# Graph layers of a four-layer network: edges from a node to itself are added from the unit's own vectors instead of being gathered

## The chip, the cores and the metric

The kernel runs on one core of a Trainium2 chip. The metric is the device time of one execution in microseconds; of the kernel before, 23 runs are shown, with a median of 2807.59 us (2790.01 to 3037.0). The core has five engines with a queue each: TensorE (PE, its weight loads shown apart as PEld), VectorE (DVE), ScalarE (ACT), GpSimd (POOL) and SyncE (SP). Transfers run on 16 DMA engines; POOL issues the gathers and SP nearly all the rest.

## The reference

The input is `x` of 8 batches x 2048 nodes x 128 features, and one adjacency matrix of 2048 x 2048 for all layers: random, symmetric, with some 16 neighbours per node, and with every diagonal element set. Four layers follow each other, attention (MHA), graph attention (GAT), MHA, GAT:

```python
_a = jax.random.bernoulli(jax.random.fold_in(_gk, 2), 0.00390625, (2048, 2048))
_a = jnp.logical_or(_a, jnp.swapaxes(_a, -1, -2))
_a = jnp.logical_or(_a, jnp.eye(2048, dtype=bool))

# MHA layer: 8 heads of 16, mask = (adj == 0), softmax over the neighbours, then
x = _layer_norm(h + (attn_out @ Wo + bo), ln1_g, ln1_b)
x = _layer_norm(x + relu(x @ W1 + b1) @ W2 + b2, ln2_g, ln2_b)

# GAT layer
h = x @ W
e = (h @ a_src)[:, :, None] + (h @ a_dst)[:, None, :]
e = jnp.where(e >= 0, e, 0.2 * e)
e = jnp.where(adj[None, :, :] == 0, -jnp.inf, e)
out = jnp.einsum('bij,bjd->bid', softmax(e), h)
x = layer_norm(out + x)          # gamma, beta
```

## The kernel before

**Units and slots.** The nodes are cut into 32 units of 64, each unit in two groups of 32. On the 128 partitions a unit is two halves of the batch (4 batches each) by 64 nodes. A unit's edges lie in 1152 slots, 9 tiles of 128: four pairs of tiles, in which each group has one tile of a pair, and a ninth tile that both groups share. The loops run over units and, in a unit, over five steps `t` (four with two tiles, one with one).

**Lists (`block_list`, `unit_list`).** For each of 16 blocks of 128 rows of the adjacency matrix, VectorE turns the row into falling column numbers (L1134), takes maxima until up to 40 neighbours of each node are listed (L1152, L1171), and a chain of small matmuls and ScalarE copies finds where each node's edges begin. For each unit, one-hot matrices `hot` (slot by node, and node by slot) are made, and for every slot the neighbour's number: `idx` (L1369), with the number of rows, 2048, where the slot is empty. A gather with the bound `nodes - 1` leaves out such rows. `empty` holds 1e30 for an empty slot and 0 for others; `owner` holds the number of the slot's node within its group. The lists are made ahead of layer 0 and between its units.

**Tables and gathers (`project`, `gather`).** As each unit leaves a layer, `project` multiplies it by the next layer's weights and stores rows in a table in HBM. A row holds one node for all 8 batches: keys and values for MHA (8192 bytes), and for GAT the score, 128 features and a one, per batch (4160 bytes). The other score of a GAT layer, which belongs to the target node, stays on chip in `t` (`spread_out`, L1665). `gather` (L1763) issues one indirect DMA per tile on POOL, 288 per layer, into a buffer of the pool `kv` (6 buffers; a GAT buffer holds four tiles).

**A GAT layer (`graph`, `opened_graph`, `after_graph`).** `opened_graph` multiplies `hot` by `t` (L2126), so that every slot has its target's score, and subtracts `empty` in `mask` (L2141 to L2150). For each step VectorE adds the gathered score and takes the leaky maximum (`score`, L2065, L2072), ScalarE takes the exponential (L2077), VectorE multiplies it into the one-hot matrix (`fold`, L2087), and TensorE multiplies the gathered features with it and sums per node in PSUM (`add`, L2103). The one in each row gives the sum of the weights as a 129th column. Even units accumulate in two of the four banks of the tile `q`, odd units in the bank `acc` and one of the three shared banks `m`. After the last step `after_graph` takes the inverse of the sums (`inverse`, L2174, L2175), scales the accumulator into `a` (L1732, L1734), multiplies the unit's own `x` by a centring matrix (`centred`, L1567: x less its mean, so that the norm needs no mean), adds the two into `r` (L2193), and goes on with `norm`, `scaled`, `keep` and `project`. The last unit of a layer goes through this in two halves.

**An MHA layer (`attention`).** TensorE spreads the queries over the slots (L1824), VectorE multiplies them with the gathered keys (L1836) and sums per head (L1843), ScalarE takes the exponential (L1853), POOL, and in some steps VectorE, weighs the values (L1869), TensorE sums per node (L1921).

**What sets the order.** No loop issues instructions. Every piece of work is an `Op` with a key (its due place), costs in us per engine that may take it, and the cells that it reads, writes, joins, holds or shares. `Plan.order` runs through the whole program once with these costs, a model of the DMA queues (bytes by a rate) and the counts of buffers, and gives each engine a fixed order; `Plan.issue` then makes the instructions in that order. A cost that is altered in one place can so alter the order of the whole program.

## Time and profile before

| | |
|---|---|
| median of 23 runs | 2807.59 us |
| profiled execution, its own time | 2799.18 us |
| its span (first to last instruction) | 2797.5 us |
| busy: PE, PEld | 2228.5 us (80%), 1359.6 us (49%) |
| busy: DVE, ACT, POOL | 2258.0 us (81%), 1474.8 us (53%), 2086.4 us (75%) |
| DMA | 1022.64 MB, mean 366 GB/s |
| gathers (software queue) | 864.44 MB, 78.2% of the 16 engines' span |
| granted TensorE clock, mean | 0.909 |

A group in the profile is a line, an engine, an operation and its operands by the program's names (`out<-in`), with their shapes, the count, the busy time, the mean of one, and the idle time of the engine just before it with the work that ended it. A stage's row gives busy time per engine, the granted clock of TensorE, the busy share of the DMA engines (by the packets' own times, so it can stand a little over 1) and the rate. fp32 matmuls are recorded as two each.

### The profile page before, as it was taken

To read this page: it belongs to the slowest core of one execution; us is meant where nothing else is said; L and a number is where in the kernel's file an instruction comes from. 1 tells how busy PE (TensorE), PEld (TensorE's weight loads), DVE (VectorE), ACT (ScalarE), POOL (GpSimd) and SP (SyncE) were. 2 spreads that over 40 slices of the span, in tenths; PEclk is the share of its full clock that TensorE was granted. 3 is DMA by queue.
4 is the path that set the end of the run, shared out by engine and by line. 5 is a ranking of instruction groups with operands and counts; after the bars stand their busy time and mean duration, and the time that the engine had idled before them with its cause. 6 is when DMAs were issued, how large, how long until landed. Compare 5 with 4: busy or idle time off the path is not lost. (4 is left out here: it accounts for less than half of the span.)

```text
span 2797.5 us, 61433 instructions
## 1 busy us (share of the span) xinstructions
PE 2228.5 (80%) x22816; PEld 1359.6 (49%) x22816; DVE 2258.0 (81%) x3674; ACT 1474.8 (53%) x4995; POOL 2086.4 (75%) x1447
## 2 busy tenths in 40 slices
PE   6568778778889886888777888888888988677775
PEld 4424443334444445666664344444444444566664
DVE  8699999989999995555555998899999998576665
ACT  6546655566555554655553354555555554454443
POOL 1188888788888877667664888788888886777774
PEclk8888999999999998999996899999999999888887
DMA  7798999889999989999998999999999997999996
GB/s 284 275 361 332 352 354 350 322 353 365 360 409 393 390 305 361 413 408 407 403 409 318 363 371 364 354 413 380 362 403 380 376 401 279 375 407 409 400 396 266
DMA packets 248067, 1022.64 MB, mean 366 GB/s; under 512 B 39184, under 2 KB 52880, under 8 KB 175856
## 3 DMA queue, kind: packets, MB, share of 16 engines
q0 software_dynamic: 166464, 864.44, 78.2%
q1 hardware_dynamic: 81296, 154.18, 14.8%
q8 instruction: 183, 3.00, 0.4%
q14 instruction: 124, 1.02, 0.1%
HBM read 978.23 MB, written 88.08 MB: 381 GB/s over the span
## 5 line engine op out<-in xcount | busy, mean ns | idle before, releaser
L1763 POOL DMA_INDIRECT kv<-table,idx x1152 | 1196.3, 1038 | 520.1 <-issue 274.1
L1869 POOL TENSOR_TENSOR kv<-kv,ex 128x2048 f32<-128x2048 f32 (+1 forms) x242 | 876.0, 3631 | 57.7 <-ACT ex L1853 53.6
L1836 DVE TENSOR_TENSOR kv<-qe,kv 128x2048 f32<-128x2048 f32 (+1 forms) x320 | 662.4, 2070 | 94.1 <-DMA kv<-table,idx 59.0
L1843 DVE TENSOR_REDUCE s<-kv 128x128 f32<-128x2048 f32 (+1 forms) x320 | 660.8, 2065 | 16.1
L1824 PE MATMUL qe<-q_sb,hot 32*128 32x512 f32 (+1 forms) x2304 | 394.3, 686 | 167.5 <-DVE kv L1836 163.8
L1921 PE MATMUL acc<-kv,hot 128*32 128x512 f32 (+1 forms) x2304 | 365.5, 650 | 69.6 <-POOL kv L1869 60.2
L2103 PE MATMUL acc_q<-kv,w 128*32 128x129 f32 (+1 forms) x4608 | 201.5, 312 | 109.5 <-DVE w L2087 97.3
L2087 DVE TENSOR_TENSOR w<-hot,e 128x512 f32<-128x512 f32 (+1 forms) x384 | 222.0, 598 | 73.0 <-ACT e L2077 59.4
L1853 ACT ACTIVATE ex<-s 128x128 f32<-128x128 f32 (+1 forms) x320 | 95.5, 299 | 313.1 <-DVE s L1843 273.7
L1824 PEld LDWEIGHTS qe<-q_sb,hot 32*128 32x128 f32 (+1 forms) x2304 | 104.5, 192 | 320.9 <-DVE kv L1836 243.8
L2103 PEld LDWEIGHTS acc_q<-kv,w 128*32 128x32 f32 (+1 forms) x4608 | 160.0, 128 | 143.4 <-DVE w L2087 114.4
L2065 DVE TENSOR_TENSOR e<-te,kv 128x16 f32<-128x16 f32 (+1 forms) x320 | 58.0, 181 | 192.8 <-DMA kv<-table,idx 190.5
L1543 ACT COPY trows<-ps_p 128x258 f32<-128x258 f32 (+1 forms) x237 | 111.3, 474 | 104.6 <-PE ps_p L1627 40.7
L1921 PEld LDWEIGHTS acc<-kv,hot 128*32 128x32 f32 (+1 forms) x2304 | 54.7, 114 | 228.3 <-issue 108.1
L2077 ACT ACTIVATE e<-e 128x16 f32<-128x16 f32 (+1 forms) x320 | 65.0, 212 | 191.0 <-DVE e L2072 183.8
L1597 PE MATMUL ps_f<-x,W 128*128 128x512 f32 (+1 forms) x264 | 147.9, 645 | 21.5 <-ACT x L1742 13.3
L2103 PE MATMUL acc<-kv,w 128*32 128x129 f32 (+1 forms) x2304 | 114.9, 299 | 57.8 <-DVE w L2087 50.1
L1581 PE MATMUL ps_y<-W,hidden 128*128 128x128 f32 x1024 | 158.4, 276 | 0.0
L1554 PEld LDWEIGHTS ps_t<-ident,normed 128*128 128x128 f32 x638 | 77.4, 154 | 126.2 <-issue 49.2
L1581 PEld LDWEIGHTS ps_y<-W,hidden 128*128 128x128 f32 x1024 | 136.8, 193 | 1.6 <-issue 1.5
L1554 PE MATMUL ps_t<-ident,normed 128*128 128x128 f32 x638 | 122.1, 313 | 17.7 <-ACT normed L1732 8.9
L1699 ACT ACTIVATE junk<-ps_y 128x128 f32<-128x128 f32 x248 | 68.8, 277 | 126.6 <-PE ps_y L1581 113.4
(221 smaller groups left out, 4122.7 us busy)
## 6 DMA issues: line engine op xcount, KB each, us to landing
x<-xd SPq DMA_DIRECT2D x96, 256.0 KB
xd<-xnew SPq DMA_DIRECT2D x93, 256.0 KB
kv<-table,idx POOLq DMA_INDIRECT x1152
table<-trows SPq DMA_DIRECT2D x128, 130.0 KB
kv<-adj_dram SPq DMA_DIRECT2D x16, 1024.0 KB
table<-trows SPq DMA_DIRECT2D x32, 512.0 KB
table<-trows SPq DMA_DIRECT2D x64, 256.0 KB
kv<-xk_dram SPq DMA_DIRECT2D x8, 1024.0 KB
```

Source lines behind the costliest of these rows:

```text
L1543: e.copy(out, in_)
L1554: e.transpose(ps.tile[:, b * P : (b + 1) * P], flat(x.tile)[:, b * P : (b + 1) * P], self.ident)
L1581: e.matmul(ps.tile[:, cols], lhsT=of, rhs=w, start=first and b == 0 and k == 0, stop=last and b == count - 1 and k == len(terms) - 1, skip ...
L1597: lambda e: e.matmul(ps.tile, lhsT=w, rhs=x.tile, start=True, stop=True),
L1763: e.indirect_dma_start(out=rows(kv.tile, j), out_offset=None, in_=self.tables[n][0:nodes], in_offset=bass.IndirectOffsetOnAxis(ap=self.idx ...
L1824: e.matmul(qe.tile[:, j, hf, :], lhsT=hot.tile[rows, t * P : (t + 1) * P], rhs=q.tile[rows, :], start=True, stop=True,)
L1836: e.tensor_tensor(k, qe.tile[:, 0:tiles].rearrange("p j h c -> p (j h) c"), k, ALU.mult)
L1843: e.tensor_reduce(s.tile[:, 0 : tiles * heads].rearrange("p (q c) -> p q c", q=2 * tiles), k, axis=mybir.AxisListType.X, op=ALU.add,)
L1869: e.tensor_tensor(v, v, w.unsqueeze(3).to_broadcast([P, 2 * tiles, heads // 2, HD]), ALU.mult)
L1921: e.matmul(out[rows, :], lhsT=hot.tile[:, col : col + GROUP * (3 - tiles)], rhs=rhs[:, 2 * j + hf, :], start=(t == 0), stop=(t == TG - 1),)
L2087: e.tensor_tensor(w.tile[:, :, j : j + tiles, :].rearrange("p x j c -> p j x c"), oh[:, j : j + tiles].unsqueeze(2).to_broadcast(shape), e ...
L2103: e.matmul(acc(b)[at : at + GROUP * (3 - tiles), :], lhsT=w.tile[:, hf * hb + b, j : j + 3 - tiles, :].rearrange("p j c -> p (j c)"), rhs= ...
```

## The change

- In the lists, VectorE multiplies the block of the adjacency matrix that lies on the diagonal by the identity and sums it, so that each node has a flag for its own edge (`seen[:, 4]`). The flag travels with the node's list and ends as `alone`: 0 with an own edge and -1e30 without.
- In `unit_list`, a second index `others` is made beside `idx`: the slot's neighbour is compared with the slot's own node, and the slot counts as empty if they agree. `empty` is made from it as well, so it now masks such slots. To compare within a unit, the nodes of its second group are numbered 33 to 64 (`number`, `target`).
- `gather` takes `others` in GAT layers and `idx` in MHA layers. The plan's bytes per tile are 113 rows for GAT instead of 120.
- In `project`, when the next layer is GAT, VectorE adds the node's two scores and `alone` into `own`. In `opened_graph` it takes the leaky maximum of it, and ScalarE the exponential.
- `inverse` adds `own` to the sum of the weights, and makes a second column, the inverse times `own`.
- `centred` becomes `mixed_products`: the unit's `x` is multiplied by a matrix of 256 columns, the layer's weights on the left and the centring matrix on the right. An even unit's products go into banks 2 and 3 of its own tile `q`, an odd unit's into two of the banks `m`.
- The addition of `r` becomes, for each batch, `a = product * (own / sum) + a`, and for each pair of batches `r = centred + a`.
- To make room, layer 2's key and value weights take layer 0's tile, both GAT layers use one tile for the turned weights and one for the 256 columns, and `ones` is narrower.

```diff
         self.empty = self.const.tile([P, self.NU, TILES], F32, name="empty")
+        self.others = self.const.tile([P, self.NU, TILES], I32, name="others")
+        self.alone = self.const.tile([P, self.NU], F32, name="alone")
+        self.own = self.const.tile([P, self.NU, self.HB], F32, name="own")
...
-        self.centre = const.tile([P, P], F32, name="centre")
+        self.turned = const.tile([P, P], F32, name="turned")
+        self.mixed = const.tile([P, 2 * P], F32, name="mixed")
+        self.centre = self.mixed[:, P:]
...
-                base=1,
+                base=1 + g % 2 * GROUP,
...
+        op({"ACT": 0.3}, lambda e: e.copy(self.mixed[:, 0:P], wx[:, 1 : P + 1]), key - 400, reads=[at], writes=[self.mixed_at])
...
         def parts(e, q):
+            if q == 0:
+                e.scalar_tensor_tensor(
+                    cand.tile.rearrange("p q c -> p (q c)"),
+                    buf.tile[:, i * P : (i + 1) * P].bitcast(I32),
+                    0.0,
+                    self.ident,
+                    ALU.not_equal,
+                    ALU.mult,
+                    accum_out=self.seen[:, 4, i : i + 1],
+                )
...
+            e.copy(aux16.tile[:, wide : wide + 1], self.seen[:, 4, i : i + 1])
...
+            e.activation(
+                self.alone[:, u : u + 1], ps.tile[:, wide : wide + 1], AF.Identity, bias=self.minus_huge, scale=1e30
+            )
...
+            other = rank.tile[:, 1]
+            e.tensor_tensor(other, rank.tile[:, 0], ps_l.tile[:, 0:TILES, DEG + 2], ALU.add)
+            own = float(self.N - u * UNIT + 1)
+            e.scalar_tensor_tensor(other, other, own, rank.tile[:, 0], ALU.not_equal, ALU.mult)
...
         def indices(e):
-            e.activation(self.idx[:, u], rank.tile, AF.Identity, bias=self.rows_n, scale=-1.0)
-            e.activation(self.empty[:, u], ps_l.tile[:, 0:TILES, DEG + 2], AF.Relu, bias=self.huge, scale=-1e30)
+            e.activation(self.idx[:, u], rank.tile[:, 0], AF.Identity, bias=self.rows_n, scale=-1.0)
+            e.activation(self.others[:, u], rank.tile[:, 1], AF.Identity, bias=self.rows_n, scale=-1.0)
+            e.activation(self.empty[:, u], rank.tile[:, 1], AF.Relu, bias=self.huge, scale=-1e30)
...
-    def centred(self, x, key, *out):
-
-        ps = self.bank("ps_c")
+    def mixed_products(self, x, key, outs, *out):
+
         count = len(self.blocks)
+        if len(outs) == 1 and count == self.HB:
+            made, pairs = outs, [lambda k=k: outs[0].tile[:, 2 + k, :].rearrange("p (b d) -> p b d", b=2) for k in range(2)]
+        else:
+            made = [self.bank("ps_c", [P, 2, 2 * P]) for _ in range(count // 2)]
+            pairs = [lambda ps=ps: ps.tile for ps in made]
+        self.mixed_in = made
 
         def run(e):
             for b in range(count):
-                cols = slice(b * P, (b + 1) * P)
-                e.matmul(ps.tile[:, cols], lhsT=flat(x.tile)[:, cols], rhs=self.centre, start=True, stop=True)
+                e.matmul(
+                    pairs[b // 2]()[:, b % 2, :],
+                    lhsT=flat(x.tile)[:, b * P : (b + 1) * P],
+                    rhs=self.mixed,
...
+                def own_scores(e, ps=ps, v=v):
+                    e.scalar_tensor_tensor(
+                        self.own[:, u, 2 * v : 2 * v + 2],
+                        rows.tile.rearrange("p (b d) -> p b d", b=hb)[:, 2 * v : 2 * v + 2, 0],
+                        self.alone[:, u : u + 1],
+                        ps.tile[:, :, P + 1],
+                        ALU.add,
+                        ALU.add,
+                    )
+
+                self.op({"DVE": 0.17}, own_scores, key, reads=[ps, rows, self.ends_at[u]], **{kind: [self.own_at[u]]})
...
+        idx = self.idx if LAYERS[n] is MHA else self.others
...
-            dma=120 * tiles * width * 4,
+            dma=(120 if LAYERS[n] is MHA else 113) * tiles * width * 4,
...
-                e.tensor_scalar(rc.tile[:, 2 * k : 2 * k + 2], sums, 1e-30, None, ALU.max)
-            e.reciprocal(rc.tile, rc.tile)
+                e.scalar_tensor_tensor(
+                    rc.tile[:, 2 * k : 2 * k + 2, 0], sums, 1e-30, own[:, 2 * k : 2 * k + 2], ALU.max, ALU.add
+                )
+            e.reciprocal(rc.tile[:, :, 0], rc.tile[:, :, 0])
+            e.tensor_tensor(rc.tile[:, :, 1], rc.tile[:, :, 0], own, ALU.mult)
...
-        ps = self.centred(mine, key, r, a)
-        op(
-            {"DVE": 0.65},
-            lambda e: e.tensor_tensor(r.tile, ps.tile, flat(a.tile), ALU.add),
+        pairs = self.mixed_products(mine, key, outs, r, a)
+
+        def residual(e):
+            for k, ps in enumerate(pairs):
+                for b in range(2 * k, 2 * k + 2):
+                    e.scalar_tensor_tensor(
+                        a.tile[:, b, :], ps()[:, b % 2, 0:P], rc.tile[:, b, 1:2], a.tile[:, b, :], ALU.mult, ALU.add
+                    )
+                cols = slice(2 * k * P, (2 * k + 2) * P)
+                e.tensor_tensor(
+                    r.tile[:, cols].rearrange("p (b d) -> p b d", b=2),
+                    ps()[:, :, P:],
+                    a.tile[:, 2 * k : 2 * k + 2, :],
+                    ALU.add,
+                )
+
+        op({"DVE": 0.5 * len(blocks)}, residual, key - 2, reads=[rc, *self.mixed_in], writes=[r, a])
```

## The prediction

> **What bounds the kernel now.** I read the page first (its forty slices show four stages of different make-up), then the busy time by stage, then the groups of instructions within one graph stage, then the packet records. The gathers start at 140 us; the last rows of a graph layer are gathered from 1056 to 1508 us (layer 1) and from 2372 to 2784 us (layer 3), by the first and last 4160-byte packet. Attention fills 140 to 1040 and 1560 to 2300. Busy time by stage (columns: PE, PEld, DVE, ACT, POOL busy, granted TensorE clock, share of the 16 DMA engines, GB/s):
>
> ```profile
> core 0: us, PE busy (x) PEld busy (x) DVE busy (x) ACT busy (x) POOL busy (x), PEclk, DMA share, GB/s
> 140.00:700.00 560.00, 436.98 (x3373) 218.31 (x3374) 524.97 (x667) 327.80 (x1054) 466.62 (x251) 0.92 0.90 348
> 700.00:1040.00 340.00, 298.75 (x2393) 151.80 (x2391) 318.12 (x234) 186.06 (x614) 290.70 (x164) 0.97 0.96 378
> 1190.00:1260.00 70.00, 58.87 (x917) 47.52 (x917) 36.15 (x131) 38.82 (x138) 45.63 (x44) 0.90 1.02 407
> 1400.00:1470.00 70.00, 55.87 (x886) 44.36 (x886) 37.20 (x132) 40.26 (x140) 47.26 (x46) 0.93 1.03 409
> 1560.00:2300.00 740.00, 641.16 (x5063) 327.76 (x5056) 676.22 (x466) 385.58 (x1276) 623.38 (x356) 0.96 0.96 378
> 2520.00:2590.00 70.00, 50.62 (x904) 42.45 (x904) 46.70 (x151) 34.41 (x137) 52.49 (x51) 0.83 1.02 408
> 0.00:140.00 140.00, 85.26 (x376) 64.40 (x376) 103.54 (x388) 82.52 (x241) 20.34 (x58) 0.85 0.74 280
> ```
>
> The reader is to see two regimes. In the graph stages the DMA engines are full (1.02 to 1.03 in every 70 us slice from 1120 to 1470 and from 2450 to 2730), and VectorE is half to two thirds busy: time there is bytes. In attention VectorE (94%, 94%, 91%) and DMA (0.90, 0.96, 0.96) are both close to full: a microsecond of either costs part of itself. The queue that carries the gathers (packets, MB, share of 16 engines), and VectorE's longest wait in layer 1 from 1120 to 1470 (total us, times, longest):
>
> ```profile
> q0 software_dynamic: 166464, 864.44, 78.2%
> ...
> DVE e L2065 <- DMA kv<-table,idx: 90.2, 62, 3.8
> ```
>
> That wait is for gathered rows. The packet records hold 69856 packets of 4160 bytes (mean 166.6 ns) and as many of 8192 bytes (mean 330 ns): 34928 rows per layer, one per edge, so a slot without an edge makes no packet.
>
> **The change, part by part.** The sum is made against the profiled execution (2799.2 us, span 2797.5); the median of the runs shown is 2807.6, 8.4 above it, and a difference worked out on the one is put on the other.
>
> *Removed rows.* Each node has its own edge, so 2048 of 34928 rows fall out of each graph layer. 2048 x 166.6 ns / 16 engines = 21.3 us per layer, 42.6 in all. The slices at 1.02 and above cover 630 of the 864 us in which graph rows are gathered, so 31.1 us surely lies on the bound; of the 11.5 at the layers' ends (shares 0.95, 0.85, 0.96, 0.64) I count seven tenths, 8. Taken: -39, bounds -42.6 and -31. The 288 gathers per layer and their 1.04 us each on POOL stay.
>
> *Lists of edges (layer 0).* Added on VectorE: one 128x128 product with a sum per block (16), between 143 ns (a sixteenth of the 2285 ns that the 128x2048 one takes) and 278 ns (a MAX8 over 128x128); I take 0.26, the nearer in size, plus 83 ns for reading the sum: 5.5 us. Two 128x9 operations per unit (32); rows 128x16, 185 and 176 ns, 128x8 from PSUM 166: 0.34 per unit, 10.9 us. By the counts of the list's rows, 8 blocks and 9 units fall before 140 us (5.8 us), the rest nearly all before 700 (10.5). ScalarE gets four small copies more (about 0.2 to 0.3 each by the 128x9 row, 302 ns); it is 59% busy there, so I count nothing; without that cover it would be 0.8 us a unit.
>
> *Own scores (in layers 0 and 2, where the next graph layer's table is made).* Two operations of 128x2 out of PSUM per unit, on VectorE; the row above them in the code, 128x8 out of PSUM, takes 158 ns, a 128x16 one 176. At 0.165 they are 10.6 us per layer. They read the finished row, so VectorE's queue waits there for ScalarE's copy, as the row above them already does (10.1 us in 15 waits); what queues behind is attention's multiply. I put nothing more on it. By the count of that row 17 units fall before 700 (5.6 us), the others after (5.0).
>
> A rule of the Trainium skill speaks against these small operations: "VectorE: DVE Perf Modes" (the section on the errata) says that each instruction pays a fixed latency and advises operands of 512 elements or more. Its row here is `rcg<-acc`, 128x2 out of PSUM, 149 ns, nearly all of it fixed. The page's own size, 120 cycles plus the columns at 0.96 GHz from PSUM and 58 from SBUF, is smaller (an estimated 127 ns and 70 ns); by it VectorE's new work in attention would shrink by about a quarter, and the sum would be about -21.
>
> VectorE thus gets 16.1 us more from 140 to 700, 15.6 more in the rest of attention and 5.8 ahead of 140. Of two nearly full resources I let the added time count by the share of idle time that the other has: DMA's 10% against VectorE's 6.3% gives 0.61, so 9.8; in late layer 0 and layer 2 (4% against 6.4 and 8.6%) about 0.35, so 5.5; at the start (26% and 26%) a half, 2.9. Sum +18.2; bounds 0 and 37.5.
>
> *The products with centre and weights side by side.* The rows of layer 1 that carry this (groups from 1120 to 1470: count, busy us, mean ns, idle before; the last two are from its timeline: start, us, line, count):
>
> ```profile
> L1625 PE MATMUL ps_p<-Wkv,xnew 128*128 128x256 f32 x215 | 66.3, 435 | 13.5 <-ACT xnew L1742 12.1 <-ACT a L1732 0.8 <-ACT trows L1543 0.4
> L1567 PE MATMUL ps_c<-centre,x 128*128 128x128 f32 x216 | 33.7, 305 | 0.0
> L2193 DVE TENSOR_TENSOR r<-ps_c,a 128x512 f32<-128x512 f32 x27 | 18.5, 687 | 6.2 <-PE ps_c L1567 6.1
> 1323.65 1.13 PE L1625 MATMUL ps_p<-Wkv,xnew 128*128 128x256 f32 x4
> 1324.62 1.05 PE L1567 MATMUL ps_c<-centre,x 128*128 128x128 f32 x8
> ```
>
> Eight matmuls of 128 columns take 1.05 us, and eight of 256 take twice 1.1: +1.1 us per unit on TensorE, with the same weight loads. Layer 1 runs 26 units (260 `ps_te` matmuls, ten each) in the 350 us from 1120 to 1470: 13.46 us each, TensorE busy 288.4, so 11.1. Afterwards it is 12.2 of 12.8 (13.46 less 0.67 for the rows): 0.6 us of slack where there is 2.4. In layer 3 it is 9.1 of 12.2 before, and 10.2 of 11.5 after. Lower bound 0: the granted clock is 0.90 to 0.95 in these slices of layer 1, and at full clock 11.1 would be 10 to 10.5. Upper bound: all of the 2.4 us slack is needed, 1.8 x 32 = 57 us. I take 0.1 us a unit, 3 us, since in late layer 0 VectorE too runs at 94% beside DMA at 0.96; the bound stays in the range.
>
> *The sums after the gather, VectorE in the graph layers.* Instead of one 128x512 addition (687 ns), four 128x128 and two 128x256 ones. The 128x256 form of the same line takes 0.41 us in the timeline, so a further 256 columns cost 0.28 and 128 take about 0.26 (an estimate from these two): 4 x 0.26 + 2 x 0.41 - 0.69 = +1.2; with two 128x4 operations (0.17 each) +1.5 us a unit. VectorE goes from 7.2 to 8.7 of 12.8 us in layer 1 and from 8.3 to 9.8 of 11.5 in layer 3: hidden under the DMA, nothing counted; uncovered it would be 48 us a layer. At the two layers' ends nothing covers it: half a unit's residual, product and small operations, +1 us each, 2 (0 to 5).
>
> *Edits with one answer, nothing:* the exponential of the own scores (ScalarE, 128x4, about 0.2 us a unit; ScalarE is 62% busy at most in the slices of the graph stages) and the constants set up on POOL and VectorE before the first rows arrive. The weights' copy into the tile that layers 1 and 3 share waits for layer 1's last product, near 1514 us, and is first needed near 2400; the key and value weights of layer 2 go into layer 0's tile, free since 140. If these covers were gone, each is one copy, below 1 us.
>
> Sum: -39 + 18.2 + 3 + 2 = -15.8 us: 2783 for the profiled execution, 2791.8 on the median, said as 2791.
>
> **The rivals.** (1) All of VectorE's new work hides, because attention is paced by the DMA: for it, in layer 2 VectorE waits 25.0 us for rows and only 9.5 for the next cause (`qe`); against it, 94% busy VectorE up to 700. -42.6 + 3: 2768. (2) None of it hides: -39 + 37.5 + 5 = +3.5: 2811. For it, early layer 0; against it, layer 2's 9% of idle VectorE. (3) The slower side: TensorE, with its PSUM banks, becomes layer 1's bound. An even unit's products now go into the other two banks of its own accumulator, which is held until the residual is made; an odd unit takes two of the three shared banks at once, while its second accumulator still has the third. Slack goes from 2.4 to 0.6 us a unit, and TensorE's queue is in order, so a late bank holds everything behind it. It decides when a unit needs more than 1.2 us of slack (0.6 plus 0.1 plus 15.8 / 32). At 1.5 us it gives +26 over the forecast: 2818; at all 2.4, 2846. For it: TensorE already waits 24.4 and 18.0 us in that stretch for `w`. Against it: those waits follow the arrival of rows, and the gated clock gives time back.
>
> The Trainium skill, "Perfetto Trace Analysis" (Identifying the Most-Contended Engine), says that matmul busy time judges TensorE's headroom badly and names the busy share of weight loads instead. That share is 0.68 in the row at 1190 and the change adds no load: by that rule rival 3 would cost nothing, and the sum would be -18.8.
>
> (4) The saving doesn't come: rows are dealt to the 16 engines by slot, the missing ones are scattered, and the fullest engine paces each gather. No gain, costs as above (+23.2): 2831. Against it: a unit has 1091 rows on average and its first eight gathers are full, so its ninth holds about 67 of 128 already, and yet the engines stay at 1.02: several gathers in flight even this out.
>
> **How the numbers follow.** The forecast 0.48, rival 1 0.15, rival 2 0.17, rival 3 0.13, rival 4 0.07. The forecast's own range is 2775 to 2805. With rival 1 below and most of 2 and 3 above, 2765 to 2822 leaves out rival 4 and the far end of 3, about two in ten with what I have not thought of. About 0.2%, 5.6 us, is what a measurement of this kernel can tell from no change. Faster: most of the forecast (0.44), rival 1, and the low ends of 2 and 3 (0.07): 0.66. Same: the forecast's upper end and the middle of 2: 0.12. Slower: 0.22. The order of all work is made anew from the altered costs; that can add some microseconds either way and is in the range.
>
> **What would show it.** 4160-byte packets: 65760 instead of 69856. Layer 1's gathers shorter by about 16 us and layer 3's by 20, DMA still at 1.0 in both. Layer 0 longer by about 13, layer 2 by 4. If DMA in layer 1 falls below 0.98 while TensorE is above 93% busy, it is rival 3; if packets fall but the stretch does not shorten and DMA sinks with TensorE no busier, rival 4. A new order that places attention's multiply badly would make the layers 0 and 2 the place of an error.

## The result, and the profile after

The changed kernel takes 2841.46 us (median of 6 runs, 2837.26 to 2844.45), the kernel before 2804.22 (47 runs): a ratio of 1.0131, 95% interval 1.0109 to 1.0154. It is 37 us slower; the forecast was 2791. Ratios and intervals, here and below, leave out executions in a second, slower state and are not simply the quotient of the two medians shown.

The profiled execution of the changed kernel has a span of 2843.9 us, 46.4 more than before. The table cuts both spans at the first and last gathered row of each layer. The column a1 is the first experiment below, the whole change with two VectorE operations formed otherwise. The forecast column holds the prediction's rounded parts, which add up to -14 instead of -15.8. Times here count from the first instruction; those of rows in the prediction count from the first packet, 10.9 us earlier, which changes no length.

| part of the span, us | before | after | a1 | forecast change |
|---|---|---|---|---|
| to the first row | 131.6 | 129.7 | 130.5 | +3 |
| layer 0 | 898.5 | 968.9 | 910.1 | +13 |
| layer 0 to 1 | 15.0 | 20.6 | 15.8 | |
| layer 1 | 452.1 | 434.3 | 434.5 | -16 |
| layer 1 to 2 | 6.8 | 17.0 | 17.0 | +1 |
| layer 2 | 839.6 | 814.4 | 821.8 | +4 |
| layer 2 to 3 | 17.4 | 17.8 | 15.7 | |
| layer 3 | 412.2 | 409.1 | 409.0 | -20 |
| last row to the end | 24.0 | 32.2 | 32.3 | +1 |

So layer 0 alone loses 70.4 us. The busy time by stage of the changed kernel (columns as before: PE, PEld, DVE, ACT, POOL busy, granted clock, share of the DMA engines, GB/s):

```profile
0.00:140.00 140.00, 83.64 (x378) 62.94 (x378) 111.87 (x424) 86.47 (x269) 21.91 (x62) 0.85 0.78 290
140.00:700.00 560.00, 411.92 (x3045) 203.56 (x3049) 536.37 (x697) 307.69 (x1005) 426.44 (x228) 0.87 0.84 318
700.00:1109.00 409.00, 344.24 (x2698) 175.17 (x2691) 383.52 (x317) 215.49 (x704) 328.35 (x184) 0.94 0.89 352
1270.00:1340.00 70.00, 59.92 (x953) 51.61 (x955) 44.60 (x176) 40.53 (x145) 50.38 (x47) 0.90 1.02 401
1600.00:2380.00 780.00, 684.27 (x5466) 342.76 (x5462) 739.71 (x565) 407.11 (x1353) 678.69 (x388) 0.97 0.99 389
2560.00:2630.00 70.00, 55.17 (x910) 45.23 (x914) 55.24 (x198) 35.14 (x145) 54.23 (x52) 0.83 1.02 396
```

In layer 0 VectorE is now 96 and 94% busy, and the DMA engines fell from 0.90 and 0.96 to 0.84 and 0.89: a microsecond of VectorE there goes nearly straight into the time (b4 below measures it). Yet the arithmetic added there is small. The groups of VectorE from 0 to 1115 us (count, busy us, mean ns, idle before) show which instructions hold the time:

```profile
L1392 DVE SCALAR_TENSOR_TENSOR rank_e<-rank_e 128x9 f32<-128x9 f32 x32 | 43.6, 1364 | 1.1
L1161 DVE SCALAR_TENSOR_TENSOR cand<-kv,ident 128x128 f32<-128x128 int32 x16 | 24.9, 1557 | 0.0
L1714 DVE SCALAR_TENSOR_TENSOR own<-trows,alone,ps_p 128x2 f32<-128x2 f32 x60 | 12.3, 206 | 1.3 <-ACT trows L1572 1.3
```

L1392 is the comparison that makes `others`, L1161 the product with the identity. A 128x9 operation of 1364 ns on average is not work: the shortest of the 32 takes 168 ns, the median one 184, the longest 5304; of the 16 of L1161 the shortest takes 280 ns, the longest 7220. Most of the time of both groups (68.5 us busy) lies in the long ones: 13 comparisons and 4 products take over 600 ns, 61.3 us together. Every one of these 17 ends within 0.16 us of the end of a multiply with which GpSimd weighs values. The timeline (start us, us, engine, line, operation) shows what a long one runs against:

```profile
385.81 7.33 POOL L1921 TENSOR_TENSOR kv<-kv,ex 128x2048 f32<-128x2048 f32 x2
386.07 7.22 DVE L1161 SCALAR_TENSOR_TENSOR cand<-kv,ident 128x128 f32<-128x128 int32 x1
393.22 0.08 DVE L1161 DVE_READ_ACCUMULATOR cand<-kv,ident 128x1 f32 x1
```

VectorE's product starts at 386.07, while GpSimd weighs values (two multiplies, 385.81 to 393.14), and ends at 393.29, 0.15 us after it. It is counted as busy throughout, and VectorE starts nothing else meanwhile. The comparison meets the same:

```profile
753.79 7.32 POOL L1921 TENSOR_TENSOR kv<-kv,ex 128x2048 f32<-128x2048 f32 x2
...
756.23 4.91 DVE L1392 SCALAR_TENSOR_TENSOR rank_e<-rank_e 128x9 f32<-128x9 f32 x1
```

It ends at 761.14, 0.03 us after GpSimd's multiplies. The Trainium skill states the rule behind it ("SBUF — State Buffer", Who interferes with whom): a VectorE instruction with two operands in SBUF contends with a GpSimd instruction that reads SBUF, over a shared port that one of them holds for its whole instruction. The rows above agree, with the end of the one 0.03 and 0.15 us after the end of the other. They add that a wait can outlast one instruction: both began under one multiply and ended with the next, which had followed directly.

In the graph layers, the rows that answer those shown of before: the gathers' queue (packets, MB, share) and VectorE's wait for rows from 1200 to 1550 us; below them the groups of the products there.

```profile
q0 software_dynamic: 166464, 847.42, 76.1%
...
DVE e L2117 <- DMA kv<-table,others: 65.4, 35, 3.5
```

All packets of the kernel, before and then after:

```profile
DMA packets 248067, 1022.64 MB, mean 366 GB/s; under 512 B 39184, under 2 KB 52880, under 8 KB 175856
```

```profile
DMA packets 248075, 1005.68 MB, mean 354 GB/s; under 512 B 43280, under 2 KB 56976, under 8 KB 175856
```

The products and the sums behind them, after:

```profile
L1664 PE MATMUL ps_p<-Wkv,xnew 128*128 128x256 f32 x216 | 59.9, 401 | 1.1 <-ACT xnew L1793 1.1
L1600 PE MATMUL ps_c<-mixed,x 128*128 128x256 f32 x112 | 26.5, 379 | 0.0
L2259 DVE SCALAR_TENSOR_TENSOR a<-acc_q,rcg,a 128x128 f32<-128x128 f32 x55 | 16.7, 344 | 6.1 <-PE acc_q L1600 5.4
L2263 DVE TENSOR_TENSOR r<-acc_q,a 128x256 f32<-128x256 f32 x28 | 11.9, 425 | 1.0
```

The queue moves 17.0 MB less, and 65760 packets of 4160 bytes stand where 69856 were: the rows are gone, as the change says. But the queue's count of packets, 166464, is the same before and after. Each row left out is recorded as a packet of 4 bytes: 30464 of these instead of 26368, 9 ns each, which are the 4096 more packets under 512 bytes. VectorE's wait for rows went from 90.2 to 65.4 us in a stretch of 350. TensorE's idle time ahead of `ps_p` went from 13.5 us to 1.1; the products of 256 columns take 379 ns each where 128 columns took 305.

### The profile page after: what moved, and what is told of

Its sections match the earlier page's. It is cut to its first block, busy times and chain, and to the rows that moved or that the text cites. A ratio compares the mean times of both kernels' runs of the same rounds, so it can differ in the third digit from the quotient of the medians.

```text
span 2843.9 us, 62415 instructions
## 1 busy us (share of the span) xinstructions
PE 2266.9 (80%) x22816; PEld 1391.0 (49%) x22816; DVE 2435.0 (86%) x4353; ACT 1497.2 (53%) x5135; POOL 2088.4 (73%) x1448
## 3 DMA queue, kind: packets, MB, share of 16 engines
q0 software_dynamic: 166464, 847.42, 76.1%
q14 instruction: 132, 1.08, 0.1%
## 4 chain that ended last, share of the span: by engine, by line
DVE 29%; PE 23%; DMA 21%; POOL 12%; issue 12%; ACT 2%; DVEq 0%; POOLq 0%; SPq 0%; ACTq 0%
DVE kv L1888 10%; DMA kv<-table,idx 10%; DMA kv<-table,others 9%; POOL kv L1921 7%; POOL kv L1815 6%; PE qe L1876 5%; DVE s L1895 4%; PE acc L1973 4%; PE acc_q L1600 2%; PE ps_t L1583 2%; PE ps_f L1636 2%; PE ps_y L1620 1%; PE acc L2155 1%; DVE cand L1171 1%; DVE w L2139 1%
## 5 line engine op out<-in xcount | busy, mean ns | idle before, releaser
L1815 POOL DMA_INDIRECT kv<-table,idx x576 | 589.2, 1023 | 315.9 <-issue 186.6
L1815 POOL DMA_INDIRECT kv<-table,others x576 | 613.2, 1065 | 240.3 <-issue 129.2
L2155 PE MATMUL acc_q<-kv,w 128*32 128x129 f32 (+1 forms) x4608 | 182.1, 295 | 62.2 <-DVE w L2139 48.0
L2155 PEld LDWEIGHTS acc_q<-kv,w 128*32 128x32 f32 (+1 forms) x4608 | 151.7, 121 | 88.4 <-DVE w L2139 55.3
L2129 ACT ACTIVATE e<-e 128x16 f32<-128x16 f32 (+1 forms) x320 | 56.9, 207 | 173.5 <-DVE e L2124 167.0
```

Source lines behind the costliest of these rows:

```text
L1815: e.indirect_dma_start(out=rows(kv.tile, j), out_offset=None, in_=self.tables[n][0:nodes], in_offset=bass.IndirectOffsetOnAxis(ap=idx[:, u ...
L2155: e.matmul(acc(b)[at : at + GROUP * (3 - tiles), :], lhsT=w.tile[:, hf * hb + b, j : j + 3 - tiles, :].rearrange("p j c -> p (j c)"), rhs= ...
```

## The experiments

Three things had to be told apart: the wait for the port (theory 1), the altered order of the whole program (theory 2), and what a removed row is worth in each graph layer.

**a1: the two list operations without the shared port.** The flag for a node's own edge is counted in the finished list of neighbours, and the comparison takes one operand from PSUM:

```diff
-            if q == 0:
-                e.scalar_tensor_tensor(cand..., buf...bitcast(I32), 0.0, self.ident, ..., accum_out=self.seen[:, 4, i : i + 1])
+            e.tensor_scalar(some.tile, aux.tile[:, 0:DEG], self.mine[:, i : i + 1], 0.0,
+                ALU.is_equal, ALU.add, accum_out=self.seen[:, 4, i : i + 1])
...
+            num = ps_l.tile[:, 0:TILES, DEG + 2]
-            e.tensor_tensor(other, rank.tile[:, 0], ps_l.tile[:, 0:TILES, DEG + 2], ALU.add)
-            e.scalar_tensor_tensor(other, other, own, rank.tile[:, 0], ALU.not_equal, ALU.mult)
+            e.tensor_tensor(num, rank.tile[:, 0], num, ALU.add)
+            e.scalar_tensor_tensor(rank.tile[:, 1], num, own, rank.tile[:, 0], ALU.not_equal, ALU.mult)
```

> The changed kernel with its two new list operations rewritten so that neither reads two operands from SBUF: the flag of the own edge is counted in the node's list (128x40, one tensor and a scalar per partition) instead of in the adjacency block, and the comparison takes its first operand from PSUM. Theory of the port: the two operations wait until POOL's weighing of the values (3.7 us each) is over, 38 + 20 = 58 us of VectorE in layer 0; here they take 0.2 to 0.3 us each, layer 0's gathers shrink from 969 to about 911 us and the time is about 2783 us. Theory of the order (the altered costs gave a worse order): layer 0 stays near 960 and the time within 10 us of 2841. Theory of sheer work (VectorE has more to do in layer 0): the same, 2830 to 2841.

Measured: 2786.7 us, 0.9929 of before (0.9903 to 0.9955). The two operations are as many as before, by the groups of a1's VectorE from 0 to 1060 us:

```profile
L1384 DVE TENSOR_TENSOR ps_l<-rank_e,ps_l 128x9 f32<-128x9 f32 x32 | 5.5, 172 | 2.1
L1385 DVE SCALAR_TENSOR_TENSOR rank_e<-ps_l,rank_e 128x9 f32<-128x9 f32 x32 | 5.4, 168 | 1.1
L1184 DVE TENSOR_SCALAR_CACHE_REDUCE some<-aux,mine 128x40 f32<-128x40 f32 x16 | 4.1, 254 | 0.6
```

The comparison takes 168 ns instead of 1364. It still runs beside GpSimd's multiplies: 17 of the 32 start while one runs, and all take 167 to 169 ns. One of them:

```profile
648.09 7.45 POOL L1914 TENSOR_TENSOR kv<-kv,ex 128x2048 f32<-128x2048 f32 x2
...
649.00 0.17 DVE L1385 SCALAR_TENSOR_TENSOR rank_e<-ps_l,rank_e 128x9 f32<-128x9 f32 x1
```

Layer 0 is 58.8 us shorter than after the change, the whole 54.8; every other part of the span stays within 8 us (table above). a1 also moves 0.3 us of cost from one entry of the plan to another, so its order is not the changed kernel's; b4 below tests the wait with the order held. Together they show the port wait as the cause of the slowdown. Without it the kernel is 17.5 us faster than before; a4 and c2 below ask how much of that is the change's.

**a2: the same two operations as entries of their own, marked for the plan** with `port=True`, the plan's word for work that meets GpSimd on the port:

```diff
+        op({"DVE": 0.35}, own_flag, key + 0.05, reads=[buf], writes=[cand], port=True)
+        op({"DVE": 0.35}, compare, key + 0.4, reads=[ps_l], writes=[rank], port=True)
```

> The changed kernel with the same two operations, each an entry of its own in the plan that is marked as needing the port shared with POOL, so that the plan gives them places where POOL is not weighing. Theory of the port: waits mostly gone (mean below 0.5 us each instead of 1.36 and 1.56), layer 0 at 905 to 930 us, time 2780 to 2800. Theory of sheer work: no change from 2841. The order is made anew here too, so by the theory of the order it could be anything from 2800 to 2860.

Measured: 2813.08, 1.0029 (1.0006 to 1.0052); layer 0 933.5. The planned places help half, and the time misses the 2780 to 2800 expected: the flag still takes 1153 ns on average, the comparison 365. Perhaps the engines' real times drift from the plan's; no run tests that.

**b4: the kernel before, with one idle operation of the same kind per unit** and the same order of all else:

```diff
+            e.scalar_tensor_tensor(self.spare, rank.tile, 1.0, rank.tile, ALU.not_equal, ALU.mult)
```

> The kernel before with one VectorE operation more per unit in the lists, 128x9 with both operands in SBUF, whose output nobody reads; nothing else differs, the order included. Theory of the port: mean 1.0 to 1.5 us instead of 0.18, 30 to 45 us of VectorE in layer 0, and the time up by 20 to 40 us (2825 to 2845). Theory of sheer work: 32 x 0.18 = 6 us, so 2804 to 2811.

Measured: 2839.25 beside 2800.43, 1.0125 (1.0082 to 1.0168): +38.8 us for 32 operations on 128x9. Its group:

```profile
L1366 DVE SCALAR_TENSOR_TENSOR spare<-rank_e 128x9 f32<-128x9 f32 x32 | 37.9, 1185 | 1.1
```

Shortest 170 ns, longest 4480. GpSimd and ScalarE run the same sequence of instructions as before, and VectorE the same with the 32 put in, so no order is altered. The 37.9 us busy and the 38.8 us longer time agree: nothing hid it (layer 0 alone is 43.3 us longer). This is theory 1 by itself, on a kernel that has nothing else of the change.

**a3: a1, but all rows gathered** (the own rows still masked and added from the unit's vectors):

```diff
-        idx = self.idx if LAYERS[n] is MHA else self.others
+        idx = self.idx
...
-            dma=(120 if LAYERS[n] is MHA else 113) * tiles * width * 4,
+            dma=120 * tiles * width * 4,
```

> As the run without port operations, but the graph layers gather with the first index, so the own rows are fetched again (and masked); everything else of the change stays. It prices the removal of 4096 rows alone. By the packets' own times: +39 us, 18 to 20 us in each graph layer. If layer 3 is no longer held by the DMA, as its 409 us against 412 suggest, then +18 in layer 1, 3 or less in layer 3, and +21 in all.

Measured: 2817.38, 1.0043 (1.0026 to 1.0060). The missing rows are worth 30.7 us in all (2817.38 less 2786.7), between the two expectations and with an order that the plan's bytes alter a little: 23.5 us in layer 1 and only 9.6 in layer 3. Of these, 6.4 and 2.1 us are lost again behind the layers' last rows (10.6 and 30.2 us in a3, 17.0 and 32.3 in a1).

**b2: a1, and in the graph layers the edges from the last 256 nodes left out too** (an eighth of the rows; the output lacks their terms):

```diff
+            e.tensor_copy(num, rank.tile[:, 1])
+            e.scalar_tensor_tensor(rank.tile[:, 1], num, 256.0, rank.tile[:, 1], ALU.is_gt, ALU.mult)
```

> The version without port operations, with the edges from the last 256 nodes left out of the graph layers too (their rows are not gathered and masked, so those terms are missing from the result). About 4100 rows per layer less, 43 us of all DMA engines. POOL pacing layer 3: layer 3 shrinks by less than 10 us (409 to about 400, the floor being 288 x 1.38 = 397), layer 1 from 434 to about 400 to 410, where POOL or TensorE stop it. DMA pacing both: 40 us less in each.

Measured: 2770.69, 0.9897 (0.9851 to 0.9942). Layer 1 went from 434.5 to 407.0 us, layer 3 from 409.0 to 405.2. Each layer gathers 4102 rows less, 42.7 us by the packets' times before (166.6 ns, 16 engines); they move layer 3 by 3.8 us: it hardly waits for bytes. GpSimd's groups of before (2450 to 2730 us) and after (2490 to 2770) had shown it:

```profile
L1763 POOL DMA_INDIRECT kv<-table,idx x199 | 215.7, 1084 | 65.5 <-issue 46.6 <-DMA kv<-table,idx 4.4 <-DVE w L2087 3.6
```

```profile
L1815 POOL DMA_INDIRECT kv<-table,others x203 | 218.7, 1077 | 61.9 <-issue 49.4 <-DMA kv<-table,others 2.7 <-DVE a L2259 1.2
```

In 280 us GpSimd issues 199 and then 203 gathers, 1.08 us each, with some 0.3 us ahead of each, most of it waiting for nothing but the issue itself: 1.38 us by 288 gathers is 397 of layer 3's 412 us. The share of the DMA engines stays at 1.02, but the rate sinks from 408 to 396 GB/s and the rows' packets lengthen (mean in layer 3 167.0 to 170.6 ns, in b2 182.1).

**b1 and c1: one more gather per unit that moves no row** (a1, all indices out of bounds). In b1 it wrote a place of the unit's own buffer, in c1 one tile that nobody reads (c1's edit):

```diff
+            if idx is self.others and tiles == 1:
+                e.indirect_dma_start(out=self.dump, in_=self.w[0]["Wq"],
+                    in_offset=bass.IndirectOffsetOnAxis(ap=self.nothing, axis=0), bounds_check=P - 1, ...)
```

> The version without port operations, with one more gather per unit in the graph layers whose indices are all out of bounds: it moves no row and costs only POOL's queue (1.08 us and the 0.3 us gap), in the same order of work. Theory that POOL's issue paces layer 3 (203 gathers in 280 us there, every gap 0.3 us and none a wait): layer 3 longer by 30 to 44 us (32 x 1.38); layer 1, whose POOL has 1.5 us a unit to spare, by 0 to 15. Theory that the DMA engines pace both: 0 to 5 in each.

> The kernel without the wait on the shared port (run a1), with one more gather per unit in both graph layers (32 each), whose indices are all out of bounds: it moves no rows, and it writes a tile that nobody reads, so nothing waits for it to land. It adds only GpSimd's time of issue. Theory A (layer 3 is paced by GpSimd, which needs 1.08 us for a gather and 0.30 us to the next): layer 3 goes from 409.0 us to 439 to 453 (32 x 1.38 = 44 us, less what its ends cover), layer 1, which is paced by the transfers, gains 0 to 20 us. Theory B (both layers are paced by the transfers, which this leaves alone): 0 to 5 us in each.

Measured: b1 3106.38, 1.1096 (1.1045 to 1.1146), layer 1 587.8 and layer 3 576.5; c1 2941.74, 1.0486 (1.0463 to 1.0509), layer 1 507.4 and layer 3 494.3. Neither tells the theories apart, since each put a second wait beside the cost of issue. GpSimd's waits, b1 from 1200 to 1500 and c1 from 2500 to 2800 us:

```profile
POOL kv L1819 <- DMA kv<-table,others: 77.6, 14, 8.9
```

```profile
POOL dump L1820 <- DMA dump<-L_Wq_dram,nothing: 18.4, 5, 4.6
POOL dump L1820 <- DVE e L2129: 8.1, 2, 4.7
```

b1's gather writes where the unit's last gather writes, c1's where the extra gather before it did, and GpSimd stands until that has landed.

**c3, d1, e1: the extra gathers write eight small tiles in turn**, so that none waits for another:

```diff
+                self.dumped += 1
+                e.indirect_dma_start(out=self.dumps[self.dumped % 8], ...)
```

> As the run with one more empty gather per unit into one tile, but the gathers write eight small tiles in turn (128x16), so that none has to wait for the one before it to land. What is left is GpSimd's time of issue alone. Theory A (layer 3 is paced by GpSimd's issue, 1.38 us a gather): layer 3 at 439 to 453 us, from 409.0 without the extra gathers, and layer 1 at 434 to 455. Theory B (both are paced by the transfers): 409 to 414 and 434 to 440.

> The kernel with one more empty gather per unit into eight small tiles in turn, beside the same kernel without these gathers (the next one) in one set. Theory A (GpSimd's issue, 1.38 us a gather, paces layer 3): layer 3 is longer by 30 to 44 us, layer 1 by 0 to 20. Theory B (the transfers pace both): 0 to 5 us each.

> The kernel with one more empty gather per unit into eight small tiles in turn. If the kernel before takes about 2804 us on this chip, as in the first three sets: theory A (each gather costs GpSimd's 1.38 us in layer 3, whatever rows it moves) gives layer 3 439 to 453 us against 409.0 without the extra gathers, and layer 1 434 to 455 against 434.5; theory B (the transfers pace both layers) 409 to 414 and 434 to 440.

Measured: e1 2839.71 beside 2804.14, 1.0124 (1.0082 to 1.0165), in a1's order of work. Layer 3 is 445.2 us, 36.1 longer than a1's; layer 1 449.3, 14.8 longer. GpSimd's waits from 2480 to 2780 us, and that stretch by engine:

```profile
POOL kv L1812 <- issue: 50.6, 166, 0.3
POOL dump L1822 <- issue: 6.1, 20, 0.3
POOL kv L1812 <- DMA kv<-table,others: 2.1, 7, 0.3
```

```profile
2480.00:2780.00 300.00, 216.52 (x3532) 178.56 (x3532) 215.73 (x772) 132.52 (x551) 233.09 (x219) 0.77 0.96 353
```

Hardly a wait but the issue is left, and DMA sinks to 0.96: layer 3 is paced by GpSimd's gathers. An extra one costs 1.13 us there and 0.46 in layer 1, where GpSimd had slack.

c3 and d1 ran on a chip on which the kernel before itself took 3028 and 3047 us, and they can be compared only there. c3 is 1.0194 (1.0138 to 1.0251) and d1 1.0216 (1.0169 to 1.0262) of before. a1, beside d1, took 3042.89, 0.9998 (0.9977 to 1.0018):

> The two list operations without the shared port, as in the first set (0.9929 of before there): 2775 to 2800 us where before is at 2804, layers 1 and 3 at 434 and 409 us.

Its layers 1 and 3 took 532.0 and 549.2 us, and GpSimd did not wait for its issue most there but for buffers, which are freed by the products of rows that came late (2600 to 2900 us):

```profile
POOL kv L1808 <- PE acc_m L2148: 56.6, 19, 8.4
POOL kv L1808 <- issue: 36.1, 112, 2.1
```

On that chip the packets of rows are longer (mean 193 ns instead of 169), the DMA share is 0.85 to 0.94, and the whole of a1 brings no gain that can be measured. The extra gathers of d1 make layer 3 37.3 us longer than d2's, as theory A said, but layer 1 39.7 longer, where 0 to 20 was expected; so there the cost isn't shown to be the issue. Why that chip differs, no run shows; the kernel before was not profiled there.

**b3: a1, with an even unit's products in the shared PSUM banks** as an odd unit's are:

```diff
-        if len(outs) == 1 and count == self.HB:
+        if False:
```

> The version without port operations, with an even unit's products put into two of the shared banks, as an odd unit's are, instead of banks 2 and 3 of its own accumulator, which is then free earlier. If holding the accumulator costs time at the layers' starts (a stretch of low DMA share from 40 to 80 us after a layer's first rows is longer than before by about 5 us): 5 us less in each graph layer, some 2777 us in all. If not, within 5 us of 2787, or slower where three shared banks are too few.

Measured: 2773.0, 0.9888 (0.9843 to 0.9933), the fastest version that gives the full output, though its interval overlaps a1's. Layer 1 is 6.4 us shorter than a1's, layer 3 3.0; in the stretch from 40 to 80 us after the first row of layer 1 the DMA share is 0.87 and 0.99 instead of 0.76 and 0.79. That fits the expectation: the even unit's accumulator was held until the residual, and gathers started late behind it. VectorE's order differs too.

> As the one before it, with the even units' products in the shared banks (0.9888 of before in its own set): 0.985 to 0.993, layer 1 shorter than in the one before it by 4 to 9 us.

On the slower chip this version was 0.9984 (0.9961 to 1.0007), with a1 at 0.9998: nothing to tell them apart. No comparable profile of d3 exists, so what was expected of its layer 1 stays open.

**a4 and c2: the order alone.** a4 is the kernel before with the costs that the changed kernel has in its plan; c2 is the kernel before with an entry that issues nothing, where the own scores stand:

```diff
+                self.op({"DVE": 0.17}, lambda e: None, key, reads=[ps, rows])
```

> The kernel before with only the costs given to the plan altered as in the change (lists, products, residual, mask, inverse, bytes per gathered tile); every instruction is as before, in an order of the plan's new making. Theory of the port: within 10 us of the kernel before, so 2794 to 2814. Theory of the order: slower by 20 us or more, with layer 0 longer by 20 or more.

> The kernel before with an entry in the plan that costs VectorE 0.17 us (where the own scores stand after the change) and issues no instruction: only the order is made anew. In all kernels with own scores layer 2 took 8 to 16 us less from the end of layer 1's gathers to the end of its own than the kernel before (846.5 us). Theory A (the shorter layer 2 is the order's doing): here too it is 8 us or more shorter. Theory B (it comes from the instructions themselves or from the rows that layer 1 no longer gathers): 844 to 849 us.

Measured: a4 2815.75, 1.0035 (1.0016 to 1.0054), layer 0 +17.2 us, layer 2 -5.9; that lies between what the two theories had expected. c2 2780.78 beside 2804.49, 0.9924 (0.9897 to 0.9951), layer 0 +9.0, layer 2 -24.9. Doing nothing in another order is a gain of 23.7 us. VectorE's wait for rows in layer 2 (1600 to 2250 us), before and in c2:

```profile
DVE kv L1836 <- DMA kv<-table,idx: 25.0, 29, 2.4
DVE kv L1836 <- PE qe L1824: 9.3, 10, 2.4
```

```profile
DVE kv L1837 <- DMA kv<-table,idx: 9.2, 17, 1.0
DVE kv L1837 <- PE qe L1825: 6.5, 21, 0.9
```

So the shorter layer 2 of the changed kernel (-25.2) and of a1 (-17.8) needs no cause in the change: the entry alone gives it. a1's whole gain over before, 17.5 us, is no larger than that.

**c4, d4, e2: b3 with the own scores entered at 0.34 us in place of 0.17**, the instructions the same:

> The fastest version so far (list operation without the shared port, even units' products in the shared banks; 0.9888 of before), with one plan cost altered: the own scores' second operation is entered at 0.34 us in place of 0.17. The instructions are the same; the order is made anew. Theory: an altered cost moves the time by up to some 25 us by the order alone, as the empty entry did (-23.7 us), mostly in layers 0 and 2: then this lies anywhere in 2755 to 2795 us, with layers 1 and 3 within 5 us of 428 and 406. If a dearer entry is itself what spreads the work of layer 2 better, layer 2 (from the end of layer 1's gathers) is at 822 us or less.

> As the one before it, with the own scores' second operation entered at 0.34 us in place of 0.17 in the plan. If an altered cost moves the time by the order alone, as the empty entry did, it is 3 to 25 us away from the one before it, most of it in layers 0 and 2; within 3 us otherwise.

> Shared banks for the even units and the own scores' second operation entered at 0.34 us. On the slow chip this was 0.7% longer than the same kernel with 0.17. If that is the order's doing it is 10 to 25 us above 2773 us here too (0.991 to 0.998 of before); if it belongs to that chip, 0.985 to 0.991.

Measured: e2 2781.93 beside 2804.14, 0.9916 (0.9885 to 0.9947), 8.9 us above b3 (the intervals overlap, and the ratio lies at the lower edge of the range expected of the order); on the slower chip c4 1.0053 (1.0025 to 1.0082) and d4 1.0056 (1.0029 to 1.0083), where b3 was at 0.9984. Layer 1 (427.9) and layer 3 (403.6) are b3's, and layer 2 is 7.0 us longer than b3's. One number in the plan again moved the time, clearly so on the slower chip alone, and a dearer entry is not what spreads layer 2 better.

## Why the prediction was wrong

**The step that failed: "Lists of edges (layer 0)".** It priced the product with the identity and the two 128x9 operations by operations of their size (0.26 and 0.34 us, 16.4 in all) and took the price as independent of what GpSimd does. The rows that set it (128x16 at 185 and 176 ns, MAX8 at 278) either ran where GpSimd weighs nothing or had at most one operand in SBUF that meets it. Measured: 75.1 us (43.6 for the comparison, 5.3 for the sum ahead of it, 24.9 for the product, 1.3 for the reading), 59 more than forecast. The sum, with one operand in PSUM, took 165 ns, as priced. Layer 0 grew by 70.4 us, and by 11.6 without the port, with 9.8 and a part of 5.5 forecast. That agrees with the weighing of VectorE against DMA, but an altered order without added work moved layer 0 by 17.2 (a4) and 9.0 us (c2), so it may be luck. b4 prices one waiting operation at 1.2 us a unit, seven times the sheer operation. The rival "None of it hides" had bounded VectorE's cost by 37.5: the bounds were set by operations too, so the range (to 2822) had no case for a wait.

The profile of before did hold a hint. The centring of `Wo` on VectorE ran twice, once in 318 ns and once in 4318. The timeline of before at the second:

```profile
515.02 4.32 DVE L1037 TENSOR_SCALAR Wo<-Wo,mean 128x128 f32<-128x128 f32 x1
515.55 3.70 POOL L1869 TENSOR_TENSOR kv<-kv,ex 128x2048 f32<-128x2048 f32 x1
```

It ends at 519.34, 0.09 us after GpSimd's multiply. It is another form (one tensor, and one scalar per partition), and it began 0.53 us before the multiply's record, so it is a hint and not the same case. The plan's code marks such work with `port=True`, and the added operations are not marked. The prediction passed over both.

**"Removed rows": -39 forecast, -30.7 measured** (a3 against a1). Layer 1 came out as said (-17.8, forecast -16), as the net of two terms: the rows gave 23.5 by a3, where 21.3 was the most by the packets, and all else cost 5.9. Layer 3 became 3.1 us shorter, not 20: 9.6 for the rows by a3, less some 6.4 for all else. The DMA share of 1.02 was read as "full, so time is bytes". Yet in layer 3 the share stayed there while rows fell away, because the mean packet lengthened (167.0, 170.6, 182.1 ns). The step said of the 288 gathers and their 1.04 us that they "stay", and left out what follows: 1.38 us with the gap, 397 of 412 us. The reading that an empty slot makes no packet was wrong as well: it makes one of 4 bytes. At 9 ns each, the 4096 of them take 2.3 us of the 42.6.

**"Own scores"** were 206 ns instead of 165 (12.3 us for 60), and layer 2 was to be 4 us longer. It was 25.2 shorter, and an empty entry in the plan alone gives 24.9 (c2). The prediction allowed "some microseconds either way" for the order; a4 and c2 show +11.5 and -23.7 for the whole. a1 takes 2786.7, c2, which removes no row at all, 2780.8: how much of a1's gain would be left under an order as good for the kernel before was not run. The rule on small operations ("VectorE: DVE Perf Modes" in the Trainium skill), which gave an estimated 127 ns for them, was farther off than the row. By that rule's figures the new work would shrink by three tenths, not by the quarter that the prediction says; its sum of -21 fits three tenths.

**"The products": +3.** TensorE did not become layer 1's bound; it is busy 59.92 of 70 us beside DMA at 1.02, and rival 3 did not happen as told. The banks that it named did cost something, 6.4 and 3.0 us (b3). The residual's pieces were 342 to 344 ns instead of 260, under cover.

**The layers' ends: +1 each forecast, +10.2 (layer 1 to 2) and +8.2 (after the last row) measured.** a1 has the same 10.2 and 8.3. With the order alone altered (a4) it is 3.8 and 3.9 already, and with all rows gathered (a3) 3.8 and 6.2. So part of it may belong to the order, and part to rows that now land earlier than the work behind them can use; which instruction holds that work was not tried.

**The rivals.** The fourth (no saving) is out: layer 1 shortened with the rows. The first (all hides) did not come about either, since the time rose; whether VectorE's sheer work hides is left open, as said of layer 0's 11.6 us. The slower side came about, by a mechanism that none of them had.

The difference of 37.3 us, split by the runs' medians: all that the change adds without the port, and the order with it, +13.2 (a3 less before, 2817.38 less 2804.2); the missing rows -30.7 (a1 less a3); the port +54.8 (after less a1). The forecast had +23.2, -39 and nothing for these. Each of the three also holds a change of order, which the runs do not part from it; only b4's +38.8 for the port is free of that.

## What to carry to other kernels

Before pricing a small VectorE operation by its size, look where its operands lie and what GpSimd runs at that time: with both in SBUF and a GpSimd multiply often beside it, 128x9 cost 1.2 to 1.4 us on average here, and 0.17 with one operand in PSUM. A DMA share of 1.0 does not say that bytes are the bound: divide the stretch by the number of gathers, and see whether the issuing engine ever waits for anything but its own issue. Where an order is planned as a whole, run the old kernel with the new costs or an empty entry first; here that alone moved the time by +11.5 and -23.7 us, as much as the change was to bring.

## What the runs showed of the hardware

A wait for the shared port is recorded as busy time of the waiting VectorE instruction, with no idle time ahead of it: only the spread (168 to 5304 ns for one shape) and the end within 0.16 us of GpSimd's multiply give it away. The wait can last over two multiplies in a row (7.22 us). A gather of 128 rows costs GpSimd 1.04 to 1.08 us and 0.30 us to the next, even if no row of it is in bounds (1044 ns in e1). A row left out by the bound still leaves a packet of 4 bytes (9 ns). And one and the same kernel took 2800 to 2804 us in four sets of runs on four chips, and 3028 to 3047 in two sets on a fifth, with the rows' packets a seventh longer in a1; a1's gain of 0.7% on one of the four was none on the fifth.
